# Four fused image layers on one core: the experts' product moved to the last image's inner loop and projection, and layer 3 of two images moved between the last image's rows' and columns' passes

## The chip, the core and the metric

The kernel runs on one core of a Trainium2 chip, in float32 throughout. The metric is the device time of one execution in microseconds; the median of three runs of the kernel before is 3649.24 us (3649.09 to 3654.0). The core's engines run side by side, each through its own instructions in its own order: PE (TensorE) multiplies matrices into PSUM, DVE (VectorE) and ACT (ScalarE) work on elements, POOL (GpSimd) here mostly issues transfers, and SP (SyncE) issues nearly all the others. Semaphores hold an instruction back until what it needs is there.

## The reference, cut to what matters

Eight images of 512 channels and 32 x 32 positions go through four layers.

- Layer 0: group norm, eight-headed attention, then three steps `h = h + 0.1 * tanh(inl_w h + inl_b)` (the inner loop), then a projection and a residual.
- Layer 1: single-headed attention over 1024 positions, with a residual.
- Layer 2: upsampling by a 12-tap filter along width and height, a leaky ReLU, downsampling in the same way.
- Layer 3: convolutions whose weights are mixed for each image from eight experts:

```python
pooled = x.mean(axis=(2, 3))
rw = jax.nn.sigmoid(pooled @ router_w.T + router_b)
out = relu(bn1(cond_conv(x, w1, rw, 1, 0)))      # W = einsum('be,eoihw->boihw', rw, experts)
out = relu(bn2(cond_conv(out, w2, rw, 1, 1)))    # 3 x 3
out = bn3(cond_conv(out, w3, rw, 1, 0))
return relu(out + x)
```

The pooled means that give an image its mixture `rw` are those of its own layer-2 output, so image b's mixed weights need layer 2 of image b to be complete.

## The kernel before, in words

Images 0 to 7 are taken one after the other through layers 0 to 2; layer 3 comes for all eight at the end. A tile of class `big` is 16 KB in each partition, and there are seven such buffers; `tmp` has six buffers of 1024 columns and four of 512 (`half`), `sums` two. PSUM has two double banks (`ps_sc`) and two pairs of single banks (`ps_tp`, `ps_mm`).

**Order of the work.** Most of the program is ordered by a planner, which takes instructions by their place in the program as soon as, by its own estimate, their inputs and a buffer are there; transfers are thus often issued long before their place in the program. In sections under `tc.manual_schedule` the named engines keep the written order. In `between`, `last_across`, `last_rows` and `last_columns` these are PE, DVE, ACT and SP; in the loop of layer 3 they are PE, DVE and ACT, and SP is left to the planner.

**Layer 0** (`layer0`): attention, then `inner`, three products of the form `product` (seven partial products P1, C11, U2, U3, C22, C21, C12 of a 2 x 2 block scheme, four matmuls each; sums T_hf of the input's quarters on DVE, L513, tanh at L692), then the projection, a fourth product of that form.

**Layer 1** (`layer1`, `weighted_rows`): scores, exponentials, and the weighted sum in the same block scheme (L1129).

**Layer 2** (class `Layer2`), in two halves e of the channels. `wide` (L1158) upsamples along one axis and writes to `across` in HBM; `turn` reads it back with the axes exchanged. `fine_passes` are the rows' passes: nine steps, in which `up` (L1188) fills both double banks, ACT multiplies by 0.2 and DVE takes the maximum (`fine`, L1194 and L1195), and `down` (L1206) of the step before goes through `sent` (L1212) to `back` in HBM. `turn_back` reads that back. The columns' passes are `narrow` (L1237) and `channels` (L1252), eight calls in all. `fine_passes` calls `fill` twice in a step, eighteen times in all. For images 0 to 6, products of the next image are called there; for image 7 there is no next image.

**The experts' product.** `Router` forms the logits from the pooled means, the gates by a sigmoid (L267), and with `operator` a matrix that mixes the experts in one matmul for seven images. `blend_early` then goes through the 34 pieces of 512 columns of the experts: a matmul (L297), a copy from PSUM by ACT and DVE in turn (L301), and a transfer from POOL to `mixed` in HBM (L302). Before, the router stands in `last_across` of image 7, and two pieces are called at each `fill` of its rows' passes; the experts come through the three buffers of the layer weights, which are free by then. `blend_last` does the same for image 7's own mixture, in nine pieces (`mix_last`, L339), inside layer 3.

**Layer 3**: `load_z` and `load_weights` fetch an image's layer-2 output and its mixed weights; `transform_weights` and `spread` prepare a 3 x 3 convolution in a form with fewer products; `c1` (L441), `c2` (L1497) and `c3` (L1515) are eight, twelve and eight matmuls; `finish` adds the residual (L1527, L1532), applies ReLU (L1535) and stores. In the loop, c1 of the next image stands between parts of c2. Before, `aside` puts the first loads, `transform_weights(0)` and c1 of image 0 between the columns' passes, and the loop runs over images 0 to 7.

Of the kernel before, what the change touches and what calls it, by code (L numbers as in the profile page):

```python
# [17 lines left out]
P = 128  # L18
# [36 lines left out]
def tile_sequence(ctx: ExitStack, tc: tile.TileContext, a: dict, out: bass.AP, shifted: bool):  # L55
# [180 lines left out]
    class Router:  # L236
# [28 lines left out]
        def gates(self):  # L265
            at = rw[:, self.images, :]
            nc.scalar.activation(at, at, AF.Sigmoid)  # L267
# [10 lines left out]
    held_experts = []  # L278

    def load_experts():  # L280
        i = len(held_experts)
        n = min(len(PARTS) * HALF, WE - i * len(PARTS) * HALF)
        if n <= 0:
            return
        t = wpool.tile([P, len(PARTS), 2, QR], F32, tag="w", name=f"experts_{i}", bufs=3)
        t = t.rearrange("p a b c -> p (a b c)")
        at = i * len(PARTS) * HALF
        nc.sync.dma_start(t[:, 0:n], a["experts"][:, at : at + n])
        held_experts.append(t)

    def blend_early():
        rows = EARLY * NR
        op = blend["early"].rearrange("p b g -> p (b g)")
        for i in range(PIECES):
            n, at = divmod(i, len(PARTS))
            ps = bank(name=f"mix_{i}")
            nc.tensor.matmul(  # L297
                ps[0:rows, :], op, held_experts[n][:, ts(at, HALF)], start=True, stop=True
            )
            t = tmp(f"mix_{i}")  # L300
            (nc.scalar.copy if i % 2 else nc.vector.tensor_copy)(t[0:rows, :], ps[0:rows, :])  # L301
            nc.gpsimd.dma_start(mixed["early"][:, ts(i, HALF)], t[0:rows, :])  # L302
            if at == len(PARTS) - 1:
                load_experts()
            yield
# [491 lines left out]
    def layer0(b, q, k, v, w):  # L797
# [148 lines left out]
        next(operators, None)  # L946
        all_of(inner)
        for it in (1, 2):
# [3 lines left out]
            for i, _ in enumerate(parts):  # L952
                for _ in range(2 if i < 4 else 0):
                    next(operators, None)
        all_of(operators)
        if b + 1 < B:
            w["q"] = weight("q", b + 1)
        else:
            load_experts()
        t = quarter_sums(f"hf_{b}_3", hf)  # L960
        all_of(product(f"proj_{b}", w["proj"], hf, t, residual(f"proj_{b}", x)))
        if b + 1 < B:
            w["k"] = weight("k", b + 1)
        else:
            load_experts()
        return x

    def layer1(b, x, w, x_next):
# [81 lines left out]
        else:  # L1050
            load_experts()
# [275 lines left out]
    def last_across(b, eT, v, inv, y):  # L1327
        two = Layer2(b)
        act, dve = nc.scalar.copy, nc.vector.tensor_copy
        router = Router(0, EARLY)  # L1330
        with tc.manual_schedule(engines=hand):
            for what, u in weighted_rows(b, eT, v, inv, y):
                if (what, u) == ("P1", 1):
                    router.sums()
                elif (what, u) == ("U2", 0):
                    router.logits()
# [346 lines left out]
```

## Time and profile before

| | us |
|---|---|
| median of three runs (lowest, highest) | 3649.24 (3649.09, 3654.0) |
| the profiled execution's own time | 3648.9 |
| its span, from first to last instruction | 3647.0 |
| PE / DVE / ACT / POOL busy | 3572.2 / 2406.2 / 1329.7 / 102.0 |
| first inner product of image 7 on PE | 3143.2 |
| router's gates of images 0 to 6 (L267) | 3306.6 |
| last `wide` of image 7 on PE | 3339.1 |
| first `up` of image 7 | 3342.0 |
| first matmul of layer 3 (c1 of image 0) | 3433.84 |
| first c2 of image 0 | 3444.26 |
| last store issued (ACT) | 3641.28 |

The mean granted clock of PE is 0.998. How the answers below are read: in a group of instructions, the columns are line, engine, operation, output and input, sizes and count, then busy time and mean duration in ns, then the engine's idle time just before them and what ended it. In a wait, the columns are total us, number and longest. A matmul of 512 float32 columns is recorded as two instructions. In the chain and the timeline a line begins with its start and its length in us.

### The profile page before, as it was taken

The numbers are of one execution on the slowest core, as the hardware profiler recorded it, in microseconds if no ns is written. First come the engines' busy times: TensorE is split into PE (matmuls) and PEld (weight loads), VectorE is DVE, ScalarE is ACT, GpSimd is POOL, SyncE is SP. The second block draws the span as 40 slices with busy tenths as digits, with TensorE's granted clock in tenths as the row PEclk, the third lists the DMA queues.
The fourth block names the chain that finished last, engine by engine and source line by source line (L and its number), as shares of the span: only waits on it lengthen the run. The fifth ranks groups of instructions, "written<-read, shape, count | busy, mean of one in ns | idle before, by whom it ended". The sixth has DMA issues, their size and how long they took to land.

```text
span 3647.0 us, 47655 instructions
## 1 busy us (share of the span) xinstructions
PE 3572.2 (98%) x19445; PEld 1751.4 (48%) x19445; DVE 2406.2 (66%) x3201; ACT 1329.7 (36%) x1772; POOL 102.0 (3%) x139
## 2 busy tenths in 40 slices
PE   8999999999999999999999999999999999999799
PEld 4346543474435643474435743465434744355243
DVE  4887568765777558765687658774687657765434
ACT  0632345223542246223452236323452235422343
POOL 4100000000000000000000000000000000001100
PEclk9999999999999999999999999999999999999999
DMA  5102440116101450015301351024401261015872
GB/s 200 50 1 84 130 162 1 45 65 198 69 1 64 133 179 1 32 53 170 122 1 64 97 174 42 1 84 130 162 1 46 66 201 64 1 43 190 311 272 108
DMA packets 139813, 348.24 MB, mean 95 GB/s; under 512 B 14720, under 2 KB 89488, under 8 KB 132800
## 3 DMA queue, kind: packets, MB, share of 16 engines
q1 hardware_dynamic: 135120, 325.96, 26.0%
q0 software_dynamic: 4320, 18.87, 1.4%
q8 instruction: 155, 2.54, 0.3%
q14 instruction: 74, 0.61, 0.1%
q10 hardware_dynamic: 144, 0.26, 0.0%
HBM read 226.55 MB, written 118.49 MB: 95 GB/s over the span
## 4 chain that ended last, share of the span: by engine, by line
PE 94%; DMA 2%; issue 1%; ACT 1%; DVE 1%; POOL 0%; SPq 0%; POOLq 0%; ACTq 0%; DVEq 0%
PE scores L827 12%; PE av L868 12%; PE inl_X L552 7%; PE inl_A L552 5%; PE av_X L1129 5%; PE inl_Y L552 5%; PE av_A L1129 3%; PE av_Y L1129 3%; PE v_X L552 3%; PE c L1497 2%; PE proj_X L552 2%; PE v_X L607 2%; PE k_X L607 2%; PE v_Y L552 2%; PE av L881 2%; PE q_X L607 2%
## 5 line engine op out<-in xcount | busy, mean ns | idle before, releaser
L846 ACT ACTIVATE e<-scores 128x1024 f32<-128x1024 f32 x504 | 516.6, 1025 | 434.4 <-PE scores L827 379.3
L827 PE MATMUL scores<-q,k 64*64 64x512 f32 x4096 | 531.9, 592 | 0.0
L868 PE MATMUL av<-e,v 64*64 64x512 f32 x4096 | 528.7, 589 | 0.0
L852 DVE TENSOR_TENSOR acc<-acc,e 128x1024 f32<-128x1024 f32 x320 | 389.3, 1217 | 37.4 <-ACT e L846 35.4
L868 PEld LDWEIGHTS av<-e,v 64*64 64x64 f32 x4096 | 156.6, 133 | 282.8 <-issue 276.8
L827 PEld LDWEIGHTS scores<-q,k 64*64 64x64 f32 x4096 | 150.4, 133 | 295.5 <-issue 220.8
L552 PE MATMUL inl_X<-T_hf,w_inl 128*128 128x512 f32 x576 | 261.6, 592 | 0.0
L1195 DVE TENSOR_TENSOR fine<-up,fine 128x1024 f32<-128x1024 f32 x128 | 150.8, 1220 | 118.8 <-ACT fine L1194 116.5
L889 DVE RECIPROCAL inv<-av 128x256 f32<-128x256 f32 x128 | 223.1, 1748 | 2.1 <-PE av L881 2.1
L692 ACT ACTIVATE inl_U<-inl_U,inl_b 128x512 f32<-128x512 f32 x96 | 66.8, 719 | 304.4 <-DVE inl_U L707 304.4
L552 PEld LDWEIGHTS inl_X<-T_hf,w_inl 128*128 128x128 f32 x576 | 108.8, 190 | 137.9 <-issue 111.7
L552 PE MATMUL inl_A<-hf,w_inl 128*128 128x512 f32 x384 | 174.6, 597 | 0.0
L1194 ACT ACTIVATE fine<-up 128x1024 f32<-128x1024 f32 x128 | 124.1, 1022 | 134.1 <-PE up L1188 121.1
L850 DVE TENSOR_TENSOR acc<-e,e 128x1024 f32<-128x1024 f32 x64 | 79.3, 1240 | 111.3 <-ACT e L846 92.3
L703 DVE TENSOR_TENSOR inl_U<-inl_X,inl_P 128x512 f32<-128x512 f32 x96 | 61.8, 685 | 109.9 <-PE inl_X L552 109.9
L1129 PE MATMUL av_A<-v,eT 128*128 128x256 f32 x512 | 122.6, 383 | 0.0
L552 PEld LDWEIGHTS inl_A<-hf,w_inl 128*128 128x128 f32 x384 | 71.5, 190 | 96.8 <-issue 86.3
L1129 PE MATMUL av_X<-v,eT 128*128 128x256 f32 x512 | 114.0, 381 | 0.0
L1016 ACT ACTIVATE eT<-scores 128x512 f32<-128x512 f32 x128 | 66.1, 602 | 115.4 <-PE scores L379 115.4
L1129 PEld LDWEIGHTS av_X<-v,eT 128*128 128x128 f32 x512 | 96.6, 190 | 19.3 <-DVE av_U L1103 6.5
L1166 ACT COPY wide<-wide 128x1024 f32<-128x1024 f32 x62 | 59.8, 1015 | 122.4 <-PE wide L1158 122.4
L1036 POOL TENSOR_TENSOR seen<-seen,acc 128x512 f32<-128x512 f32 x16 | 20.3, 1269 | 3006.6 <-DVE acc L1028 3006.0
(377 smaller groups left out, 5562.2 us busy)
## 6 DMA issues: line engine op xcount, KB each, us to landing
x<-in_x_dram SPq DMA_DIRECT2D x64, 512.0 KB, 9.3
across_u<-wide SPq DMA_DIRECT2D x128, 256.0 KB, 3.7
turned<-across_u SPq DMA_DIRECT2D x64, 512.0 KB, 5.9
back_u<-sent SPq DMA_DIRECT2D x256, 128.0 KB, 2.3
back<-back_u SPq DMA_DIRECT2D x32, 1024.0 KB, 7.6
w_v<-stored_u_v SPq DMA_DIRECT2D x14, 1792.0 KB, 7.4
out_dram<-z SPq DMA_DIRECT2D x31, 512.0 KB, 2.8
spill_u<-z SPq DMA_DIRECT2D x28, 512.0 KB, 5.9
```

The source lines that it names most:

```text
L552: nc.tensor.matmul(dst, lhs, rhs, start=(opens and s == 0 and cc == 0), stop=(cc == 1 and s == rows), skip_group_check=True,)
L607: nc.tensor.matmul(dst, lhs, rhs, start=(what in opens and s == 0 and cc == 0), stop=(cc == 1 and s == rows), skip_group_check=True,)
L827: nc.tensor.matmul(ps[r][rows[c]], k[rows[r], oc, jc * P + c * HD : jc * P + c * HD + HD], q[rows[r], oc, ts(sh, HALF)], start=True, stop= ...
L846: nc.scalar.activation(e, pair, AF.Exp, scale=HD ** -0.5)
L850: nc.vector.tensor_add(accs[g], exps[t - 1], e)
L852: nc.vector.tensor_add(accs[g], accs[g], e)
L868: nc.tensor.matmul(avs[g][r][rows[c]], v[rows[r], jc, ts(2 * oc + c, HD)], e[rows[r], ts(c, HALF)], start=(jc == 0), stop=(jc == SC - 1),)
L881: nc.tensor.matmul(ps[rows[r]], ones[:, 0:HD], acc[:, ts(r, HALF)], start=True, stop=True)
L889: nc.vector.reciprocal(copies[g][:, at], totals[g][:, at])
L1129: nc.tensor.matmul(ps[:, ts(s, QR)], left[:, j, at : at + P], right[:, j, :], start=(what in ("P1", "U2", "C22") and s == 0 and j == 0), s ...
L1194: nc.scalar.mul(t, ps, 0.2)
L1195: nc.vector.tensor_max(t, ps, t)
```

## The change

- `gates` computes the sigmoid as 1 / (1 + exp(-t)): an Exp on ACT, an addition and a reciprocal on DVE.
- The router of images 0 to 6 moves from `last_across` to layer 0 of image 7, after the first two parts of the first inner product. `blend_early` follows: its experts are loaded into `big` tiles of eight pieces, two of them ahead; one piece is called after each of the seven parts of the second and third inner products, three after each part of the projection. All PSUM copies are on ACT. `load_experts` and its calls are gone.
- `last_across` begins with the loads of image 0's z and of the weights of images 0 and 1, and ends with the load of image 1's z. It is now called after the layer weights' pool is closed and layer 3's pool is open.
- A new generator `lean` does layer 3 of one image in steps: c1 in four, c2 in four, c3 with residual, ReLU and store in four (14 steps with two empty ones for image 0, 13 with one for image 1). One step is called at each of the eighteen `fill` places of the rows' passes and after each of ten places of the columns' passes. Its PSUM banks are single ones of `ps_mm`, and each output quarter is finished in two halves.
- Loads of z and weights of image 2 come between rows and columns. The loop of layer 3 runs over images 2 to 7; the loads of `blend_last`, c1 of image 2 and the loads for image 3 stand at its head; `mix_last` pieces are called two and one in each image.

```diff
         def gates(self):
             at = rw[:, self.images, :]
-            nc.scalar.activation(at, at, AF.Sigmoid)
+            nc.scalar.activation(at, at, AF.Exp, scale=-1.0)
+            nc.vector.tensor_scalar_add(at, at, 1.0)
+            nc.vector.reciprocal(at, at)
...
+        for _ in range(2):
+            load()
+        yield
         for i in range(PIECES):
-            n, at = divmod(i, len(PARTS))
-            ps = bank(name=f"mix_{i}")
+            ps = bank(ps_tp, f"mix_{i}")
+            n, at = divmod(i, BLOCK)
             nc.tensor.matmul(
-                ps[0:rows, :], op, held_experts[n][:, ts(at, HALF)], start=True, stop=True
+                ps[0:rows, :], op, tiles[n][:, ts(at, HALF)], start=True, stop=True
             )
+            if at == BLOCK - 1:
+                load()
             t = tmp(f"mix_{i}")
-            (nc.scalar.copy if i % 2 else nc.vector.tensor_copy)(t[0:rows, :], ps[0:rows, :])
+            nc.scalar.copy(t[0:rows, :], ps[0:rows, :])
             nc.gpsimd.dma_start(mixed["early"][:, ts(i, HALF)], t[0:rows, :])
...
+        mixing = iter(())
+        if b + 1 == B:
+            router = Router(0, EARLY)
+            router.sums()
+            router.logits()
+            router.gates()
+            router.operator(blend["early"])
+            mixing = blend_early()
+            next(mixing)
         all_of(inner)
...
+                next(mixing, None)
...
-        all_of(product(f"proj_{b}", w["proj"], hf, t, residual(f"proj_{b}", x)))
+        for _ in product(f"proj_{b}", w["proj"], hf, t, residual(f"proj_{b}", x)):
+            for _ in range(3):
+                next(mixing, None)
+        all_of(mixing)
...
+            zs[0] = load_z(0)
+            for i in range(2):
+                wts[i] = load_weights(i)
...
             two.turn(1)
+            zs[1] = load_z(1)
         return two

+    def last_rows(two, chain):
         with tc.manual_schedule(engines=hand):
+            two.fine_passes(lambda: next(chain, None))
+
+    def last_columns(b, two, chain):
         with tc.manual_schedule(engines=hand):
             z = big_tile(f"z_{b}", [P, CC, S])
+            steps = [(two.narrow, 0, 0), (two.narrow, 0, 1), (two.channels, 0, 0, z),
+                     (two.channels, 0, 1, z), None, None, (two.narrow, 1, 0), (two.narrow, 1, 1),
+                     (two.channels, 1, 0, z), (two.channels, 1, 1, z)]
+            for step in steps:
+                if step is not None:
+                    step[0](*step[1:])
+                next(chain, None)
+            all_of(chain)
         return z
...
+    def lean(b):
+
+        transform_weights(b)
+        for g in range(2):
+            ps = bank(name=f"c1_{b}_{g}")
+            src = wts[b][:, 0:C].rearrange("p (cc o) -> p cc o", o=P)
+            for cc in range(CC):
+                nc.tensor.matmul(
+                    ps, src[:, cc], zs[b][:, cc, ts(g, HALF)], start=(cc == 0), stop=(cc == CC - 1)
+                )
+                if cc == 1:
+                    yield
+            inner_rim(b, g, ps)
+            if g == 1:
+                spreads[b] = spread(b)
+            yield
+        yield
+        if b == 0:
+            yield
+        main, odd = (bank(name=f"c2_{b}_{i}") for i in range(2))
+        one, two = tmp(f"one_{b}"), tmp(f"two_{b}")
+        h2 = tmp(f"h2_{b}", S)
+        c2(b, main, 1, True, False)
+        nc.scalar.copy(one, main)
+        yield
+        c2(b, odd, 3, True, True)
+        yield
+        c2(b, main, 2, False, False)
+        nc.scalar.copy(two, main)
+        nc.vector.scalar_tensor_tensor(one, one, 2.0, two, ALU.mult, ALU.subtract)
+        nc.vector.tensor_add(one, odd, one)
+        nc.scalar.activation(h2[:, ts(1, HALF)], one, AF.Relu, bias=bn[1][1], scale=bn[1][0])
+        yield
+        c2(b, main, 0, False, True)
+        nc.scalar.activation(h2[:, ts(0, HALF)], main, AF.Relu, bias=bn[1][1], scale=bn[1][0])
+        yield
+        for oc in range(CC):
+            scale, bias = bn[2][0][:, oc : oc + 1], bn[2][1][:, oc : oc + 1]
+            dst = zs[b][:, oc, :]
+            apart = dst.rearrange("p (n i) -> p i n", i=2)
+            at = C + 12 * P + oc * P
+            for i in (1, 0):
+                ps = bank(name=f"c3_{b}_{oc}_{i}")
+                nc.tensor.matmul(
+                    ps, wts[b][:, at : at + P], h2[:, ts(i, HALF)], start=True, stop=True
+                )
+                nc.vector.scalar_tensor_tensor(
+                    apart[:, i], ps, scale, apart[:, i], ALU.mult, ALU.add
+                )
+            nc.scalar.activation(dst, dst, AF.Relu, bias=bias)
+            nc.sync.dma_start(out[b, ts(oc, P), :], dst)
+            yield
...
+    two = last_across(B - 1, *last)
+    chain = lean_images()
+    last_rows(two, chain)
+    zs[2] = load_z(2)
+    wts[2] = load_weights(2)
+    zs[B - 1] = last_columns(B - 1, two, chain)
     mixing = blend_last()
+    next(mixing)
     redo = None
     engines = mybir.EngineType
     with tc.manual_schedule(engines={engines.PE, engines.DVE, engines.Activation}):
+        for g in range(2):
+            c1(LEAN, g)
+        transform_weights(LEAN)
+        spreads[LEAN] = spread(LEAN)
+        zs[LEAN + 1] = load_z(LEAN + 1)
+        wts[LEAN + 1] = load_weights(LEAN + 1)
...
-        for b in range(B):
+        for b in range(LEAN, B):
...
-            next(mixing, None)
+            for _ in range(2):
+                next(mixing, None)
...
-            if b:
-                next(mixing, None)
+            next(mixing, None)
```

## The prediction

> **What bounds the kernel now.** I read first the page's busy table, then the windows of the last image, then its waits, then the chain of work at the end.
>
> ```profile
> PE 3572.2 (98%) x19445; PEld 1751.4 (48%) x19445; DVE 2406.2 (66%) x3201; ACT 1329.7 (36%) x1772; POOL 102.0 (3%) x139
> ```
>
> TensorE (PE) is busy 98% of 3647.0 us, so moving work helps only where PE stands still. The windows (columns: PE, PEld, DVE, ACT, POOL busy, PE clock, DMA share, GB/s) show where:
>
> ```profile
> 3338.00:3434.00 96.00, 66.20 (x437) 19.37 (x438) 41.95 (x54) 36.54 (x54) 18.95 (x35) 0.95 0.96 341
> 3140.00:3242.00 102.00, 102.00 (x267) 44.59 (x260) 71.95 (x109) 23.37 (x39) 0.00 (x0) 1.00 0.05 18
> 3434.00:3628.00 194.00, 193.93 (x498) 81.45 (x496) 80.50 (x115) 73.99 (x95) 0.00 (x0) 1.00 0.56 209
> ```
>
> From 3338 to 3434 (the last image's rows' and columns' passes, with the experts' product) PE is busy 66 of 96 us while the DMA engines are at 96%. In the inner loop and projection (3140 to 3242) PE is full and DMA idle (5%). Layer 3 (3434 to 3628) keeps PE full. The waits of PE in 3338 to 3434:
>
> ```profile
> PE mix L297 <- ACT mix L301: 15.0, 11, 2.7
> PE narrow L1237 <- DMA back<-back_u: 7.1, 2, 5.9
> PE mix L297 <- DVE mix L301: 3.2, 6, 0.9
> ```
>
> The `mix` copies in turn wait for their buffer; the groups of that window say for what:
>
> ```profile
> L297 PE MATMUL mix<-experts,blend_early 128*112 128x512 f32 x68 | 35.7, 628 | 18.2 <-ACT mix L301 15.0 <-DVE mix L301 3.2
> L301 ACT COPY mix<-mix 112x512 f32<-112x512 f32 x17 | 10.0, 590 | 28.8 <-DMA mixed_u<-mix 22.5 <-PE mix L297 6.3
> ```
>
> So the stage is held by DMA: 39 MB pass between 3330 and 3445 at 340 GB/s. Chain, for the pitch of matmuls (start, us, what):
>
> ```profile
> 3475.07 6.87 PE c L441 x16
> 3481.94 2.58 PE c L1497 x6
> 3484.52 0.99 PE mix_last L339 x8
> 3485.51 7.07 PE c L1515 x16
> 3492.58 2.58 PE c L1497 x6
> ```
>
> Each fp32 matmul of 512 columns is two records, 6.87 / 16 = 0.429 us each, 0.859 a matmul. `c` L1497 starts an image at 3466.16 and the next at 3492.58: 26.42 us an image, two `mix_last` pieces (0.99 each) among them, so 24.44 without.
>
> **What the skill says.** "ScalarE: Activation LUTs", section "Table sets: the hidden batching unit": exp followed by tanh needs one table load, both being in one set. The trace agrees: its loads are 8 at L422, 8 at L769 and one of 1283 ns at L267 (Sigmoid), none at the Tanh of L692. "DMA: Bandwidth & Descriptors", section "Issuing engines are not separate DMA queues": queues share the same 16 engines. The trace agrees: 7.8 MB of POOL's and 31.3 MB of SP's together fill them, and the row writes, 2.3 us to landing over the whole run, take 8.9 there. "Perfetto Trace Analysis", section "Tensor Engine Instruction (MATMUL, LD_WEIGHTS)": VectorE and ScalarE run strictly in order, and matmul ends are modelled; I therefore use pitches on PE and orders of program on DVE and ACT. "TensorE: Matmul & The Clock Gate", section "Why this matters for your kernels": an idle PE falls to half clock; the clock of 0.74 in 3420 to 3440, after the 5.9 us wait, agrees.
>
> **The change, part by part** (against the profiled execution, 3648.9 us; the median is 3649.24, so 0.3 is added at the end).
>
> *Experts' product into the inner loop and projection.* 34 pieces x 0.859 = 29.2 us of PE, now where PE has no room: +29.2. Their 34 ACT copies (20.1 us) lie beside 23.4 of 102 us of ACT. POOL issues (0.53 each) find POOL empty. DMA: 8.9 MB of experts and 7.8 MB written, into a stage at 18 GB/s. In the projection three pieces come per part, each 2.0 us apart (3.43 + 2.58 over 3); a `half` buffer is held for copy 0.59, issue 0.53 and a landing of some 4 us (estimate, from 3.7 us of the across writes), and four buffers give a piece per 1.3 us: hidden. Uncovered (6.1 us landing, as in the jam) it is 1.8 us: still hidden.
>
> *Router earlier.* On DVE: sums 1.1, logits 0.6, operator 3.6 (3331.6 to 3335.2), and in place of the Sigmoid an Exp (0.25, as L267's), an add (0.2, as the 128x56 at L254) and a reciprocal (at most 0.4: L889's 1748 ns for 256 columns, scaled): 6 us. DVE is 72 of 102 us there, but the T_hf sums that open the next product are late already (5 waits of 4.8 us in total there). If all 6 us land ahead of them PE loses 6; but the planner can put pieces of the product, which need nothing else, into that gap and into the old 4.8 us. Bounds -4 to +6; I take 0. The Sigmoid's load of 1.3 us goes from an ACT that had 10 us idle there: 0.
>
> *Rows and columns with layer 3 of images 0 and 1.* Before, from the first `up` (3342.0) to the first layer-3 matmul (3433.84): 91.8 us. After, PE has: 8 `up` and 8 `dn` of 1.04 (16.6), four `narrow` of 1.1, four transposed channels of 0.88, and two images of 28 matmuls (24.05 each): 72.6. To that I add gaps by order on ACT and DVE, with durations of the groups: Relu 1.12, `z` halves 0.75 (L1527), `fine` 1.0 on ACT and 1.2 on DVE, pitches.
>  - Step 3: image 0's segments 5 and 6 are empty, so step 2 holds 2.1 us of PE; the DVE does rim's wait (0.9), four spreads (2.7), then two `fine` (2.4): `up` 3 starts 6.1 after `up` 2. Gap 4.0.
>  - Steps 5 and 6, two output quarters each: per step ACT does 2 `fine`, Relu, one or two `sent`, Relu, each Relu behind two `z` halves that stand behind two `fine` on DVE: about 8.3 us against 5.5 of PE, some carried over. Gaps 1.4 + 2.8.
>  - Second `narrow`: its banks wait for copies behind image 1's spread: 3.8.
>  - Image 1's `two` copy and h2: 1.6.
>  Rows: 47.5 + 8.2 = 55.7; columns: 25.1 + 5.4 = 30.5; together 86.3. After the last `dn`, 19 us of PE stand before the third `narrow`; writes and the read back of `back` need about 14.4 (copies 1.1, issues 2.7, landings 2.5 and 8), so the old 7.1 us wait is covered; without cover it costs up to 7. DMA there is back 4.2 + 2.1 (first read) + outputs 2.1 + loads of z and weights, some 17 MB in 56 us even if the next stage's loads come early, against 39 MB in 115. Lower bound 72.6 (no gap), upper 100 (every step at 8 us, and the wait for back).
>  Here: 86.3 - 91.8 = -5.5.
>
> *Layer 3's own loop* starts at image 2: two periods less, -2 x 24.44 = -48.9. The nine `mix_last` pieces stay, three an image. Their experts, z_3 and weights_3 are asked for only at the loop's head: 4.2 + 2.1 + 1.1 MB, at 340 GB/s 22 us, while PE reaches c1 of image 3 after 6.9. But SP's order outside hand-ordered sections is not program order: image 7's x, used from 3240, was issued at 3025 as soon as a buffer was free:
>
> ```profile
> 3025.40 2.25 SPq L86 DMA_DIRECT2D x<-in_x_dram  x4
> ```
>
>  With seven big buffers, of which z_1, z_2, z_7, two `back` hold five in the columns, the loads can start there. I take +2 of up to +14.
>
> *z_0, weights 0 and 1 in front of the across pass on SP*: 10 issues, 4.3 MB, ahead of the first across write (3315.9). The buffer of the spent sums is free at about 3280; at 340 GB/s they are done by 3295: 0. If that buffer came 30 us late, everything behind it on SP would.
>
> Sum: +29.2 + 0 - 5.5 - 48.9 + 2 = -23.2; 3648.9 - 23.2 + 0.3 = 3626.
>
> The sum checks against idle: before, 91.8 less PE's need there (29.2 + 16.6 + 7.9) leaves 38; after it is 13.7 + 2.
>
> **Rivals.**
> 1. *Loads at layer 3's head come late.* SP holds them behind image 1's outputs; c1 of image 3 waits 22 - 7 = 15 us instead of 2: 3639. For: they stand late in the program; against: the early x. Chance 0.14.
> 2. *Back comes late.* Loads put early share the engines, and `narrow` waits again, 7 to 10 us: 3634. For: 8.9 us landings in the jam; against: half the rate of bytes. Chance 0.08.
> 3. *PE-bound throughout.* Gaps of 3 instead of 13.7, inner waits filled (-4): 3612. For: PE full in layer 3 and in the earlier images' passes; against: empty segments and order on DVE are fixed by hand. Chance 0.06.
> 4. *Slower: the passes serialise.* Image 0's steps sit in the same in-order queues as `fine` and `sent`; if each of nine steps waits for the other's chain (PE segment, two `z`, Relu, then `sent`), a step lasts 13 us, not 6.2: 117 + 30.5 = 147.5, so 3626 + 61 = 3687. It decides at a window of 91.8 + 48.9 - 29.2 - 2 = 109.5, that is, 8.8 us a step. Against: only two of nine steps have that chain twice, and I get 8.3 for these. Chance 0.05.
> 5. *Nothing gained*: window near 109 by a mixture of 1, 2 and 4. Chance 0.04.
>
> **Numbers.** Likeliest case 0.63, alone 3617 to 3634. Under 3613 lies most of rival 3; above 3640 rivals 4, 5 and a part of 1. Range 3613 to 3640. About 0.2% (7.3 us) is what a measurement of this kernel can tell from no change. Faster 0.91 (likeliest, 1, 2, 3), same 0.04, slower 0.05.
>
> **What will show it.** Right: PE full through the inner loop, 29 us longer from its start to the end of the projection; no `mix` wait on a DMA; about 86 us from the first `up` to c1 of image 2; the gap ahead of the fourth `up`; DMA share well under 0.96 there; six periods of about 25 to 27 us. Wrong: PE waiting for T_hf by several us after the first product; `narrow` waiting for `back`; c1 of image 3 waiting for z or weights; steps of the rows over 8 us; a `sent` write held on SP behind a load without buffer.

## The result, and the profile after

| | before | after |
|---|---|---|
| median of six runs (lowest to highest), us | 3652.91 (3649.09 to 3656.84) | 3639.36 (3637.48 to 3642.02) |
| span of the profiled execution, us | 3647.0 | 3638.4 |

The ratio is 0.9965, with a 95% interval of 0.9954 to 0.9977: the kernel is 13.5 us faster by the medians. The forecast was a sum of -23.2 us and a time of 3626. The time fell inside the range, but the gain is little more than half of what the sum gives, so the sum has to be taken apart.

That is done by stages on PE, each cut at a matmul that both kernels have: the first `inl_A` of image 7, the first `xT` of its layer 1, the first `up`, the c1 that opens layer 3's loop, and the router's matmul for image 7, just ahead of the loop's first c2.

| stage, us | before | after | difference | forecast |
|---|---|---|---|---|
| start to the first `inl_A` | 3143.2 | 3144.7 | +1.5 | 0 |
| inner loop and projection, to layer 1 | 137.0 | 172.2 | +35.2 | +29.2 |
| layer 1 and across, to the first `up` | 61.8 | 61.5 | -0.3 | 0 |
| passes, to the loop's c1 | 91.7 | 92.2 | +0.5 | -5.5 |
| head of layer 3 | 10.3 | 13.3 | +3.0 | +2 |
| rest of layer 3 | 203.0 | 154.4 | -48.6 | -48.9 |
| span | 3647.0 | 3638.4 | -8.6 | -23.2 |

The missing 14.6 us lie in three rows: 6.0 in the inner loop, 6.0 in the passes, 1.0 in the head. Another 1.5 us come ahead of anything that was changed. Of these, 1.4 lie between the inner loops of images 5 and 6: behind a wait of 1.9 us for `sent`, PE had a mean clock of 0.74 (2571.0 to 2577.5), where another execution (e3 below) had 1.00 behind a wait of 1.5. Over all the kernels below this start varies between 3142.5 and 3148.5, so stages are compared first and whole times only within a few us. (The medians differ by more than the spans because the profiled execution of before, 3648.9 us, was one of its shorter ones.)

The engines' busy times in the profile after:

```profile
PE 3575.7 (98%) x19445; PEld 1753.4 (48%) x19445; DVE 2396.9 (66%) x3194; ACT 1337.6 (37%) x1788; POOL 102.1 (3%) x139
```

PE has the same 19445 matmul records as before, and 3.5 us more of busy time in a span that is 8.6 shorter: no work was saved, it was packed closer, and some of it ran slower. The windows (PE, PEld, DVE, ACT, POOL busy; PE clock; DMA share; GB/s) show where:

```profile
3140.00:3242.00 102.00, 98.79 (x265) 41.90 (x258) 67.64 (x124) 33.45 (x56) 7.93 (x15) 0.98 0.28 99
3378.00:3471.00 93.00, 82.83 (x465) 29.33 (x466) 49.45 (x63) 42.85 (x57) 0.00 (x0) 0.94 0.75 256
3484.00:3620.00 136.00, 135.32 (x364) 56.61 (x363) 56.70 (x82) 53.17 (x67) 0.00 (x0) 1.00 0.53 195
```

The inner loop is no longer full: 98.79 of 102 us, at a clock of 0.98, where before had 102.00 at 1.00. The passes have gone from 66 of 96 us at a DMA share of 0.96 to 83 of 93 at 0.75: they are no longer held by DMA. Layer 3's loop is full as before, and its pace too. The chain of what ended last (start, us, what):

```profile
3508.20 2.58 PE c L1484 x6
3510.77 1.85 PE mix_last L343 x16
...
3527.41 0.99 PE mix_last L343 x8
...
3535.47 2.58 PE c L1484 x6
```

From c2 to the next image's c2 there are 27.27 us with three pieces of `mix_last` (1.85 + 0.99) among them: 24.43 without, the period of before. The waits of PE from 3340 to 3500 (total us, number, longest):

```profile
PE c L1581 <- DVE z L1584: 3.3, 2, 2.0
PE narrow L1248 <- DVE narrow L1253: 3.1, 1, 3.1
PE up L1199 <- DVE fine L1206: 2.6, 1, 2.6
PE c L445 <- DMA z<-spill_u: 1.9, 3, 1.5
...
PE c L1484 <- ACT two L1566: 0.7, 1, 0.7
```

The old waits for `mix` copies (18.2 us) and for `back` (7.1) are gone. The transfers of the experts' product now land in 2.8 us, 6.1 before. What is left are the four places that the forecast named, and a wait for image 3's z at the head. They make 11.6 us, less than the 13.7 + 2 that I gave them. So the passes are not longer than forecast because of more waiting; matmuls themselves took longer. The timeline of PE after (start, length, record, and in brackets the wait ahead of it):

```profile
3378.47 2.33 PE L1199 MATMUL up<-turned,up_v 32*64 32x512 f32 x16 [1.11 <-ACT wide L1177]
3380.73 4.29 PE L1545 MATMUL c<-z,weights 128*128 128x512 f32 x8
...
3386.00 1.98 PE L1545 MATMUL c<-z,weights 128*128 128x512 f32 x4
3387.91 1.09 PE L1217 MATMUL dn<-fine,dn_v 64*32 64x512 f32 x16
...
3395.59 3.13 PE L1199 MATMUL up<-turned,up_v 32*64 32x512 f32 x16 [2.61 <-DVE fine L1206]
3398.65 4.71 PE L1484 MATMUL c<-spread,weights 128*128 128x512 f32 x6
...
3404.31 2.84 PE L1484 MATMUL c<-spread,weights 128*128 128x512 f32 x6
3407.08 1.11 PE L1199 MATMUL up<-turned,up_v 32*64 32x512 f32 x16
...
3444.64 1.68 PE L1248 MATMUL narrow<-back,dn_h 64*32 64x512 f32 x16 [3.12 <-DVE narrow L1253]
```

By pitch, from one start to the next, the same `up` takes 1.04 us at 3407, 2.26 at 3378 and 3.06 at 3395; the same six records of `c` take 2.77 at 3404 and 4.64 at 3398. The granted clock in these stretches is 0.51 (3378.5 to 3380.7), 0.85 (3380.7 to 3384.9), 0.50 (3395.6 to 3398.6) and 0.59 (3398.6 to 3403.3). "TensorE: Matmul & The Clock Gate", section "What's actually happening", says that an idle PE is throttled to half its clock, that release takes some 3.4 us of activity, and that the window which decides is free-running, so that the same kernel is hit differently from run to run. The traces agree with the half (0.50, 0.51) and with the chance, as the table of the experiments shows. I had cited this page for the clock of before, and then put no price on it.

### The profile page after: what moved, and what is told of

Its sections match the earlier page's. It is cut to its first block, busy times and chain, and to the rows that moved or that the text cites. A ratio compares the mean times of both kernels' runs of the same rounds, so it can differ in the third digit from the quotient of the medians.

```text
span 3638.4 us, 47658 instructions
## 1 busy us (share of the span) xinstructions
PE 3575.7 (98%) x19445; PEld 1753.4 (48%) x19445; DVE 2396.9 (66%) x3194; ACT 1337.6 (37%) x1788; POOL 102.1 (3%) x139
## 4 chain that ended last, share of the span: by engine, by line
PE 95%; DMA 2%; DVE 1%; ACT 1%; SPq 0%; issue 0%; DVEq 0%; ACTq 0%
PE scores L831 12%; PE av L872 12%; PE inl_X L556 7%; PE av_X L1140 5%; PE inl_Y L556 5%; PE inl_A L556 5%; PE av_A L1140 3%; PE av_Y L1140 3%; PE v_X L556 3%; PE c L1484 2%; PE proj_X L556 2%; PE v_X L611 2%; PE k_X L611 2%; PE v_Y L556 2%; PE av L885 2%; PE up L1199 2%
## 5 line engine op out<-in xcount | busy, mean ns | idle before, releaser
L707 DVE TENSOR_TENSOR inl_U<-inl_X,inl_P 128x512 f32<-128x512 f32 x96 | 61.8, 685 | 112.3 <-PE inl_X L556 112.3
L1140 PEld LDWEIGHTS av_X<-v,eT 128*128 128x128 f32 x512 | 96.6, 190 | 19.3 <-DVE av_U L1114 6.5
L1140 PEld LDWEIGHTS av_A<-v,eT 128*128 128x128 f32 x512 | 92.4, 190 | 10.0
```

The costliest lines, as they stand in the source:

```text
L1140: nc.tensor.matmul(ps[:, ts(s, QR)], left[:, j, at : at + P], right[:, j, :], start=(what in ("P1", "U2", "C22") and s == 0 and j == 0), s ...
```

## Experiments

The stage times of all of them, in us, from their profiles; medians and ratios to the kernel before, measured beside each, follow with each experiment.

| kernel | start | inner | across | passes | head | loop |
|---|---|---|---|---|---|---|
| after | 3144.7 | 172.2 | 61.5 | 92.2 | 13.3 | 154.4 |
| e1 router late | 3145.5 | 171.9 | 61.5 | 92.6 | 14.7 | 154.2 |
| e2 empty steps filled | 3143.7 | 170.5 | 61.5 | 93.6 | 13.9 | 154.4 |
| e3 one empty step | 3142.5 | 172.2 | 61.6 | 89.2 | 15.6 | 153.8 |
| e4 experts' move alone | 3145.3 | 172.2 | 61.6 | 62.1 | 15.3 | 204.1 |
| e5 router first | 3144.7 | 166.6 | 61.5 | 92.2 | 13.4 | 154.2 |
| e6 loads early | 3144.1 | 173.3 | 61.6 | 89.6 | 12.8 | 156.1 |
| e7 steps between `wide` | 3145.8 | 173.3 | 62.3 | 87.9 | 19.3 | 154.4 |
| e8 e3, e5, e6 and e7 | 3145.5 | 166.6 | 62.3 | 93.7 | 14.0 | 154.3 |
| e9 router first, head | 3147.5 | 166.6 | 61.5 | 92.1 | 10.3 | 155.3 |
| e10 e9 and e3 | 3145.9 | 166.6 | 61.5 | 87.9 | 10.3 | 155.2 |
| e11 e10 and e7's steps | 3148.5 | 166.6 | 62.3 | 86.4 | 11.4 | 155.4 |
| e12 sigmoid | 3142.7 | 172.2 | 61.5 | 89.7 | 15.1 | 154.6 |

Two things bear on how this table is read. First, after, e1, e5, e6, e9 and e12 have the same waits in the passes (3.3, 3.1, 2.6 and 0.7 us), and their passes take 89.6 to 92.6; the seven kernels with the same 3.2 us wait of `inl_A` in the inner loop take 170.5 to 173.3 there. Differences of up to 3 us in these two columns are therefore no effect of an edit by themselves, and a claim on them rests on waits that are gone or new. Second, in e4, e7, e8 and e11 the loop's c1 starts ahead of the last ten transposes of the columns, so that 1.7 us (e4) or 1.1 us (the others) of the columns' work stand under head.

### The experts' move alone (e4)

```diff
-    LEAN = 2
+    LEAN = 0
```

With it go the loads of image 2 between the passes and those of the next image at the head; the loop runs over all eight images.

> Only the experts' product is moved; layer 3 of all eight images stays in the loop behind the columns' passes, with nothing between the passes. Theory (the first part alone adds 29 us or more to a full PE and takes less than that from the passes, which are then held by their own chain of ACT, DVE and the write and read of back; the second part is what pays): rows about 41 us, columns about 22 with the wait for back in full, 63 instead of 92.4, but 49 more in the loop: 92.4 - 63 = 29 less, 49 more, some 2 to 3 of half clock: 3639 + 20 to 23 = 3659 to 3663, slower than before by 7 to 10. Rival (the passes were held by DMA alone, and the experts' move is the gain): rows under 30 us, total 3640 to 3648.

Median 3660.29 (3658.51 to 3662.76), ratio 1.0025, interval 1.0014 to 1.0037: slower than before, as the theory had it. The inner loop and projection have the same 172.2 as after; the passes fall to 62.1 without the product; the loop is back at 204.1. So the experts' move by itself loses: 35.2 us are paid in a stage that was full, and passes and head together give back 24.6 (102.0 before, 77.4 here). In the head, the router's matmul for image 7 waits 2.3 us for its sums. The two steps of layer 3 then put 2 x 24.05 us of PE's work ahead of the loop and lengthen passes and head together by only 28.1 us (77.4 to 105.5), while the loop gives back 49.7. What PE waits for without them:

```profile
PE up L1199 <- DVE fine L1206: 8.0, 7, 2.4
PE dn L1217 <- ACT sent L1223: 4.0, 2, 2.5
```

These are waits for `fine` in seven places and for `sent` in two, and layer 3's matmuls go into them.

### Where the router's six microseconds are paid (e1, e5)

In the trace after, PE stops once in the inner loop:

```profile
3156.24 3.38 PE L556 MATMUL inl_A<-hf,w_inl 128*128 128x512 f32 x4 [3.19 <-DVE hf L693]
3159.42 0.51 PE L259 MATMUL router<-parts,ones 128*128 128x56 f32 x2
3159.73 3.84 PE L556 MATMUL inl_X<-T_hf,w_inl 128*128 128x512 f32 x8
```

The next product's P1 and the router's matmul stand ahead of U2 (`inl_X`) in PE's order; before, U2 followed without a pause. The wait is 3.19 us, and then four records take 3.18 where they take 1.72 elsewhere. e1 moves the whole router block behind the first inner product, by moving the call that ends it:

```diff
+        all_of(inner)
         if b + 1 == B:
             router = Router(0, EARLY)
...
             next(mixing)
-        all_of(inner)
```

> The router of images 0 to 6 comes after the first inner product instead of into it; nothing else changes. Theory (the router, put ahead, made the planner set the next product's P1 and the router's matmul in front of U2 on PE, where P1 waited 3.2 us for hf and PE then ran at half clock for 1.7 us more): the first inner product to the end of the projection takes 132.8 - 5 = about 128 us, no wait of inl_A on hf, total 3634 to 3635 against 3639.4. Rival (VectorE has 6 us of router to do somewhere, and what it delays only moves): the 3.2 us wait turns up as a wait on T_hf in the second product, the stage stays at 132 to 133 us, total 3639.

Median 3639.66 (3636.97 to 3647.17), ratio 0.9971, interval 0.9962 to 0.998. The stage has 171.9: nothing was gained, and the rival held. The first turn of the products is as before, and the wait stands at the next one:

```profile
3177.80 1.90 PE L556 MATMUL inl_X<-T_hf,w_inl 128*128 128x512 f32 x2 [3.15 <-DVE T_hf L517]
```

Here it is for T_hf itself, on a DVE with the router's instructions among the sums. e5 puts the block to the start of image 7's layer 0, ahead of the attention, with a bank of `ps_tp` for its logits:

```diff
+        if b + 1 == B:
+            router = Router(0, EARLY)
+            router.sums()
+            router.logits()
+            router.gates()
+            router.operator(blend["early"])
...
-            router = Router(0, EARLY)
-            router.sums()
-            router.logits()
-            router.gates()
-            router.operator(blend["early"])
```

> The router of images 0 to 6 stands at the start of layer 0 of image 7, ahead of the attention, where DVE is busy 9 to 11 of 20 us; its logits use a single PSUM bank. Theory (the inner loop's stage is 5 to 6 us longer than 29.2 us of product explain, because 6 us of router on DVE delay either hf or T_hf by 3.2 us, and half clock follows): neither wait appears, the time from the first inner product to the transposes of layer 1 falls from 172.2 to 167 or 168 us; total 3634 to 3635. Rival (the pieces of the product themselves, by their copies on ACT and the order of PE, cost the 5 us): the stage stays at 171 to 172 us, total 3639.

Median 3636.68 (3634.25 to 3639.72), ratio 0.996, interval 0.9945 to 0.9975. The stage falls to 166.6, 29.6 above before, and U2 is back behind the first two parts of its product without a wait:

```profile
3152.89 3.60 PE L556 MATMUL inl_X<-T_hf,w_inl 128*128 128x512 f32 x8
```

So the move of the 34 pieces costs 29.6 us there, and the router's place another 5.6. In the trace after, 5.2 of these can be seen: the wait of 3.2, 1.5 us of slow P1, 0.3 for the router's matmul and 0.25 of slow U2. DVE's sums for U2 were ready at the same moment in after and e5 (the last T_hf ends at 3155.6 in each); what differs is the planner's order on PE, in after with P1 first. That the router's place makes it choose so is shown by e1, which keeps the bank that e5 changes, and by e5; why it does, was not tried.

The new place is not free either. From image 6's first inner product to image 7's there are 421.0 us in all five kernels that have the router ahead of the attention, and 419.1 in the other nine. At its start DVE and ACT have the router, the first exponential comes late, and PE stops:

```profile
3029.07 1.09 PE L878 MATMUL av<-e,v 64*64 64x512 f32 x8 [1.05 <-ACT e L856]
```

So e5 moves the router from a place where it costs 5.6 us to one where it costs 1.9; the gain is 3.7. In the whole, where the ratio goes from 0.9965 to 0.996, it is not clear of the noise.

### The Sigmoid put back (e12)

```diff
-            nc.scalar.activation(at, at, AF.Exp, scale=-1.0)
-            nc.vector.tensor_scalar_add(at, at, 1.0)
-            nc.vector.reciprocal(at, at)
+            nc.scalar.activation(at, at, AF.Sigmoid)
```

> The changed kernel with the Sigmoid of before in place of Exp, addition and reciprocal. Theory (Exp shares a table with Tanh, Sigmoid does not): two more table loads of 1283 ns inside the inner loop, the gates' matrix ready 1.5 to 2 us later, the inner stage 0 to 3 us longer than 172.2. Rival (the planner hides the loads, or Sigmoid's set holds Tanh too): one load or none there, the same stage time.

One execution: 3637.81, the inner stage 172.2 as after. ACT has three more table loads than after, 1.28 us each: at 3152.4 and 3482.2 at the gates of the two routers, and at 3290.0 at layer 1's exponentials (L1027). Those of the gates as a group:

```profile
L267 ACT ACT_TABLE_LOAD x2 | 2.6, 1283 | 0.0
```

Inside the inner loop there is one load, not the two that the theory gave: the Tanh behind the gates needs none, so the rival held. This load lies in ACT's idle time, five us ahead of the gates (3157.8). The other form of the sigmoid brings nothing that can be seen here. (The passes of this kernel, 89.7, differ from those of after with no edit there; head and passes together are 104.8 against 105.5.)

### The gap ahead of the fourth `up`, and the half clock (e2, e3)

e2 puts one and two spare matmuls into image 0's two empty steps, into a bank that nobody reads:

```diff
-        yield
-        if b == 0:
+        for n in (1, 2) if b == 0 else ():
+            for i in range(n):
+                ps = bank(name=f"warm_{n}_{i}")
+                nc.tensor.matmul(ps, ident, zs[b][:, 0, 0:HALF], start=True, stop=True)
+            yield
+        if b:
             yield
```

> Image 0's two empty steps get one and two spare matmuls of 512 columns (2.6 us of useless PE work in a gap of 2.6 us); their results are read by nobody. Theory (after the 2.6 us wait before the fourth up, PE runs at half clock: that up took 3.13 instead of 1.04, the c2 part after it 4.64 instead of 2.77): both return to 1.04 and about 2.8, the stage from the first up to c1 of image 2 shortens from 92.4 to about 88.5, total 3635. Rival (these matmuls were long for another reason, such as a late operand): up and c2 stay at 3.1 and 4.6, the stage is 92.4 or, with the spare work in the way, up to 93.

Median 3637.71 (3636.26 to 3639.36), ratio 0.9965, interval 0.9951 to 0.9979: no change in the whole. In its place the edit did what the theory says:

```profile
3394.48 2.00 PE L1199 MATMUL up<-turned,up_v 32*64 32x512 f32 x16
3396.41 2.84 PE L1484 MATMUL c<-spread,weights 128*128 128x512 f32 x6
```

From the third `up` to the end of the first c2 group there are 9.7 us (3389.45 to 3399.19) instead of 12.4 (3390.85 to 3403.29), although 3.0 us of useless matmuls were put in: the wait of 2.6 is gone, and `c` has its full pace. The fourth `up` still needs 1.93 at a granted clock of 1.00, 0.9 more than the usual 1.04: its second double bank is freed by the later of two `fine`, and this wait is inside the group, where the list of waits doesn't show it. So of its 2.0 us of excess after, 0.9 is the bank and 1.1 the clock. But the stage as a whole has 93.6. The half clock came elsewhere in this execution: the first c1 took 5.64 in place of 4.29, and behind the second `narrow`, after the same 3.1 us wait, `c` took 4.70 where after had 2.84. A gap thus costs its length and, by chance, up to some 3 us more.

e3 removes one of the two empty steps, so that image 0's c2 starts a place earlier:

```diff
-        if b == 0:
-            yield
```

> Image 0 has one empty step instead of two, so each later step comes one place earlier. Theory (the gap at the fourth up comes from steps that give PE nothing, and is paid twice, as a wait and as half clock): c2's first part fills the gap after waiting some 1.5 us for the spread, no half clock follows; the stage shortens from 92.4 to 87 to 88, total about 3635. Rival (the row step is held by ACT and DVE, and PE's empty steps only show it): the gap moves to the spread before c2, 2.5 us and half clock again; the stage stays within 1 us of 92.4, total 3639.

Median 3638.1 (3635.32 to 3640.6), ratio 0.9964, interval 0.9952 to 0.9975. The gap at the fourth `up` is gone from the waits and the passes have 89.2 (-3.0). The head has 15.6 (+2.3):

```profile
PE c L445 <- DMA z<-spill_u: 3.6, 1, 3.6
```

The stage that got shorter ran into the same load of z; most of the gain was given back. That the shorter passes are the edit's work this trace alone does not show, since e12 has 89.7 and 15.1 without it; e10 below does.

### The loads for the head (e6), and steps between the `wide` (e7)

After, the DMA share is 0.27 from 3400 to 3420 and 0.99 from 3440 to 3460:

```profile
3400.00:3420.00 20.00, 18.74 (x107) 5.84 (x107) 9.53 (x11) 8.90 (x12) 0.00 (x0) 0.94 0.27 70
...
3440.00:3460.00 20.00, 16.20 (x76) 6.92 (x74) 6.50 (x10) 5.44 (x9) 0.00 (x0) 1.00 0.99 340
```

The loads of `last_experts` come first on SP, from 3449, and z of image 3 last, at 3473. e6 sets them by hand: z of image 2, its weights and the experts at the ninth, eleventh and sixteenth `fill`, and z and weights of image 3 at the fifth place of the columns' passes.

```diff
+    def early_loads(n):
+        if n == 9:
+            zs[2] = load_z(2)
+        elif n == 11:
+            wts[2] = load_weights(2)
+        elif n == 16:
+            next(mixing)
...
+                if at == 4:
+                    zs[3] = load_z(3)
+                    wts[3] = load_weights(3)
```

> The loads of z_2 and weights 2 stand at the fifth and sixth step of the rows' passes, the first loads for mix_last at the eighth, those of z_3 and weights 3 in the middle of the columns' passes, all in the written order of SP. Theory (the stage between passes and loop takes 13.3 instead of 10.3 us because the DMA engines, idle at 3400 to 3420, are full from 3440 on and z_3 comes last): the head falls to 10.3 to 10.5 us, the passes stay within 1 us of 92.2, total 3636 to 3637. Rival (the bytes only move and now meet the writes and reads of back): narrow waits for back by 3 us or more, passes 95 or longer, total 3639 or more.

Median 3639.4 (3637.49 to 3645.53), ratio 0.9968, interval 0.9956 to 0.998: nothing in the whole. The wait for z is gone, and the next one is behind it:

```profile
PE router L259 <- DVE parts L254: 2.4, 1, 2.4
```

Image 7's sums for the router stand on DVE behind the spreads of the loop's first c2, and PE's router matmul waits for them; the six records of c2 behind it have a pitch of 4.45 instead of 2.75, which is the loop's 1.7 us more. e7 takes two of `lean`'s steps forward, one after each of the last two `wide`:

```diff
             two.wide(1, 1, y, (act, dve))
+            next(chain)
             two.wide(1, 0, y, (act, dve))
+            next(chain)
             two.turn(1)
```

> Image 0's first two steps (half a c1 each) stand after each of the last two wide calls, where PE waits 1.1 us twice for ACT's copies; all later steps come two places earlier. Theory (these two waits are followed by half clock: the first up took 2.33 instead of 1.04 and the c1 after it 4.29 instead of 3.4): both waits and the half clock go, 2.2 + 2.1 us; the empty steps and their gap stay, one place earlier; from the end of the weighted sum to c1 of image 2 some 4 us less, total 3635. Rival (ACT and DVE are the limit there, and transform and rim in front of the copies put off the first up by what was gained): the same time, 3638 to 3640.

Median 3643.49 (3640.22 to 3646.83), ratio 0.9976, interval 0.9967 to 0.9985: by the medians some 4 us slower than after. Across and passes have 150.2 instead of 153.7; without the 1.1 us of transposes that count to the head here, that is 2.4 us less, where some 4 were expected. The head has 19.3:

```profile
PE c L445 <- DMA z<-spill_u: 5.6, 1, 5.6
```

e3, e12 and e7 thus show the same beside after: with the loads where the planner puts them, passes and head together take 104.8, 104.8 and 107.2 against 105.5, and what the passes save is waited for at the head.

### Everything at once (e8)

All four edits together, of which these lines are the core:

```diff
-        if b == 0:
-            yield
...
+            router = Router(0, EARLY)
...
+        elif n == 16:
+            next(mixing)
...
             two.wide(1, 1, y, (act, dve))
+            next(chain)
```

> All four together: router ahead of the attention, loads in the passes, two steps between the wide calls, one empty step less. Theory (each removes another wait with its half clock, 5 + 3 + 4 + 3): 3639.4 - 15 = 3624 to 3626. Rival (the row steps with c3 are held by DVE, and what is taken away elsewhere returns as waits on z, as it did with one empty step, where they grew from 3.3 to 4.7 us): 3630 to 3633.

Median 3638.47 (3638.05 to 3641.37), ratio 0.9966, interval 0.9952 to 0.9979. Theory and rival both fell: it is no better than after. The inner loop has its 166.6, but the passes 93.7, with waits that were not there:

```profile
PE dn L1218 <- ACT sent L1224: 5.5, 1, 5.5
PE narrow L1249 <- DMA back<-back_u: 3.7, 2, 2.4
```

Both stand behind writes to `back` that landed late. The wait for `back`: on SP, the experts of `mix_last` were issued from 3437.9 to 3442.1, and only then the last write to `back`, whose copies had ended at 3438.9; its four transfers were issued from 3442.6 and landed by 3455.1, and `back` was read from 3455.6. The wait of `dn`: writes issued from 3423.6 on stand behind a read of `back`, two outputs and the weights of image 2, landed from 3433.9 on, and until then ACT had no `sent` buffer. Loads put early by hand lie ahead of the writes in the same queue in both cases: kin to the hazard that the prediction named for `sent`, made here by my own edit. That the weights caused the wait of `dn` is not shown by itself: e11 below, without them there, has a wait of the same kind of 3.1 us.

### The same without the experts' loads in front (e9, e10, e11)

e9 is e5 with z of image 2 at the ninth `fill`, z and weights of image 3 in the columns' passes, the experts left to the planner behind the columns, and image 7's sums ahead of c1 of image 2:

```diff
+                if done == 9:
+                    zs[2] = load_z(2)
...
+                if at == 4:
+                    zs[3] = load_z(3)
+                    wts[3] = load_weights(3)
...
+        router = Router(B - 1, 1)
+        router.sums()
```

> Router ahead of the attention; z_2 loaded at the fifth step of the rows, z_3 and weights 3 in the middle of the columns ahead of the experts of mix_last; at the head of layer 3 the router's sums of image 7 stand ahead of image 2's spread. Theory (the head has two limits one behind the other: z_3, and behind it the sums that wait on DVE for the spread, 2.4 us when z_3 was early): the head falls from 13.3 to 10.5 to 11 us with neither wait, the inner stage stays at 166.6, the passes within 1.5 us of 92.2; total 3636.7 - 2.5 = 3634. Rival (the experts of mix_last now come last and PE waits for them before the second c2 part): a wait of mix_last of 2 us or more, total 3636 to 3638.

Median 3635.34 (3632.31 to 3637.68), ratio 0.9956, interval 0.9942 to 0.9969. The head is 10.3, as before the change: its 24 records of c1 at 0.429 and nothing else. e10 takes out the empty step as well:

```diff
-        if b == 0:
-            yield
```

> As e9_head with one empty step less. Theory (with the head no longer waiting for z_3, the 3 us that one empty step less gains in the passes are kept): passes 89 to 90, head 10.5 to 11, total 3630 to 3632. Rival (the passes' gain is handed back to the next thing that comes at its own time, back or mix_last's experts): head or narrow wait 2 to 3 us more, total 3634.

Median 3631.01 (3627.36 to 3634.05), ratio 0.9946, interval 0.9932 to 0.9959. The passes are at 87.9, below all six kernels with the old waits (89.6 to 92.6), and now the head stays at 10.3: e3's gain, which was handed back there, is kept here. The waits of e10:

```profile
PE c L1592 <- DVE z L1595: 2.7, 1, 2.7
PE narrow L1249 <- DVE sent L1224: 1.3, 1, 1.3
...
PE mix_last L343 <- DVE blend_last L277: 0.9, 1, 0.9
```

The second `narrow` no longer waits (3.1 in after); the first now waits 0.8 and, inside its group, the 1.3 shown. No load is waited for. Against after, by the stages: -5.6 in the inner loop, -4.3 in the passes, -3.0 at the head, +0.8 in the loop (its first piece of `mix_last` waits 0.9 for its mixture), +1.2 at the start (the router's 1.9 is in it): 3627.4 against 3638.4. It is 20.7 us faster than before and, across two measurements, some 7 (by the ratios) or 8.3 (by the medians) faster than after: the version to take. (The two intervals of the ratio, e10's up to 0.9959 and that of after from 0.9954, overlap a little; but all five executions of e10 lie below all six of after, and the waits and stages tell them apart.) e11 adds e7's two steps to it:

```diff
             two.wide(1, 1, y, (act, dve))
+            next(chain)
             two.wide(1, 0, y, (act, dve))
+            next(chain)
```

> As e10_head_empty with two of image 0's steps between the wide calls. Theory (each wait ahead of the first up and its half clock go): across and passes together some 3 us less than in e10_head_empty, total 3628. Rival (the steps taken from the columns leave too little ahead of the third narrow, and it waits for back, as with all four changes together, where it waited 3.7 us): 3631 to 3634.

Median 3631.11 (3629.09 to 3632.44), ratio 0.9943, interval 0.9928 to 0.9958: the same as e10. The passes have 86.4, or 87.5 with the transposes that count to the head here; the head is then 10.3 as in e10, across takes 0.8 more, and a `dn` now waits 3.1 us for a `sent` on ACT.

## Why the prediction was right and wrong, point by point

Two terms of the sum failed: the router, put at 0, and the passes, whose matmuls were priced at full pace.

**Right.** The direction, and the two large terms: the loop -48.6 (forecast -48.9), the 34 pieces 29.6 in e5 (29.2). Copies, POOL's issues and landings are hidden, as said: PE waits for nothing in e5's inner loop. z of image 0 and weights of 0 and 1 ahead of the across pass cost nothing (61.5 against 61.8). That the Sigmoid's table load is worth 0 held in e12.

**Wrong: "Router earlier", taken as 0.** It is 5.6, near the upper bound of +6. The step said that the T_hf sums were late already, by 4.8 us in five waits, and that the planner could put pieces of the product into this and the new gap. The first is a misreading: in the trace of before PE is busy 102.00 of 102 us there and never waits for T_hf; only its weight loads do, six times, 1.5 us in all. So there was no old gap to fill, and nothing to gain the -4 of the bounds from. And the pieces need the operator, which DVE finishes at 3165.1, nine us after the end of the gap that the router made in after; the first `mix` comes at 3178.9, and even in e5, with the operator long ready, at 3173.5. I filled a gap with work that needs the very result that makes the gap. e1 shows that the next turn-over has no room either, e5 that ahead of the attention the router costs less, 1.9.

**Wrong: the passes, -5.5, measured +0.5.** The gaps were right in place and near in size: at the fourth `up` 2.6 + 0.9 inside the group (4.0 forecast), at z 3.3 (4.2), at the second `narrow` 3.1 + 0.6 inside (3.8), at `two` 0.7 (1.6); 11.2 for 13.7. The failing term is the 72.6 us of PE work, which I took at full pace. First, the half clock: from the pitches above, 1.2 at the first `up`, 0.6 at c1, 1.1 at the fourth `up` and 1.9 at c2, together 4.8. Second, the alternation: four records of `c` have a pitch of 1.91 beside `up` and `dn` and 1.72 among their like, six of them 2.77 and 2.58. That is 0.19 for each of fifteen groups, and 0.10 for three that have such a neighbour on one side only, 3.2 us. "TensorEngine Tiling (Array Packing)", section "Key Properties", says that changing the tiling mode drains the TensorE; it gives no figure, and the trace's is this 0.19, if it is that drain, which no run tested apart. 72.6 + 11.2 + 4.8 + 3.2 = 91.8, against 92.2. Both terms could have been seen: the trace of before had the clock of 0.74, and in its chain, beside `up`, the pitch of 1.91 for four records:

```profile
2526.76 1.04 PE up L1188 x16
2527.80 1.91 PE k_A L607 x4
```

**The head, +2, measured +3.0** of its bounds up to 14: 1.9 us of waiting for z, and the rest in matmuls that run slower behind it. The size was fair, but treating the term as a constant was not: it takes back what the passes gain (e3, e7), and leaves only when the loads are placed and image 7's sums stand ahead of c1 (e6, e9, e10).

**The rivals.** The time came out at rival 1's 3639, for another reason: c1 of image 3 waits 1.9 us, not 15. Rival 2 is out: `narrow` waits for no `back`. Rival 3 is out, PE is not full. Rivals 4 and 5 are out: the passes have 92.2, and 4 decides from 109.5. That the time fell inside the range is luck: the range reached to rival 1, whose cause did not occur.

What stays open: why the planner puts P1 ahead of U2 when the router is there, and which gaps are followed by half clock in a given execution.

## What to carry to other kernels

Work moved into gaps of another kind of matmul should be priced with the gaps that remain, each with up to some 3 us of half clock behind it, and with the changes of tile size, here 0.19 us a group. Before a step is put into a full stage, look at what its result is needed for: it must run where the engine has room and early enough that the work meant to cover it can start. And when a stage is shortened, look first at the load that its successor waits for, and move only loads whose place in the queue has no urgent write behind it.

## What the runs showed of the hardware

After waits of only 1.1 us twice in a row (3375 and 3378) the granted clock was 0.51, and after one of 2.6 us it was 0.50; in e10 the same pair of waits of 1.1 us was followed by an `up` of 1.36 us and a c1 at full pace. After the 3.1 us wait at the second `narrow`, the clock stayed at 1.00 in after and `c` was slow in e2. So the length of a gap alone does not decide it, and six kernels with the same waits in the passes took 89.6 to 92.6. In e8 SP's transfers landed in the order of their issue from 3405 to 3475: a write to `back` issued at 3442.6 landed 11.6 us later, behind eight loads, where the median over the run of after is 2.2. A wait for the second of two banks inside one group (0.9 us at the fourth `up`) does not appear in the list of waits; it shows only in the pitch.
